# A scan ahead of an out-projection, copies ahead of casts, scans ahead of taps: three reorderings in a two-layer sequence kernel

## The chip, the cores and the metric

The kernel runs on one core of one Trainium2 chip. The metric is the device time of one execution in microseconds (us); of several executions the median is given. Five engines work side by side, each on a queue of its own in strict order: TensorE (PE, matrix products and transposes, with its weight loads shown as PEld), VectorE (DVE), ScalarE (ACT), GpSimd (POOL) and SyncE (SP, which issues the transfers). They wait for each other through semaphores. Operands lie in SBUF; products land in PSUM, which has eight banks here.

## The reference, cut to what matters

Two layers over 2 × 1024 tokens of width 512. Each layer is an attention-like block and a feed-forward block, each with a residual addition and a layernorm behind it:

```python
x = layernorm(x + mamba(x))        # in-projection, 4-tap causal convolution, decayed scan, gate, out-projection
x = layernorm(x + ternary(x))      # out = (x @ W) * scale; out *= tanh(|out|)/|out|, norm held under 0.99
x = layernorm(x + recurrence(x))   # below
x = layernorm(x + swiglu(x))       # (silu(x @ Wg.T) * (x @ Wu.T)) @ Wd.T, integer weights, 512 -> 2048 -> 512
```

The recurrence, in which most of the change lies:

```python
y    = gelu(x @ w_y + b_y)
xb   = x @ w_x + b_x;  conv = conv_b + sum_k conv_w[k] * shift(xb, k)
gx   = sigmoid(conv @ w_ig + b_ig);  ga = sigmoid(conv @ w_ag + b_ag)
a    = exp(-8 * ga * softplus(a_param));  mult = sqrt(1 - a*a)
h[t] = a[t] * h[t-1] + gx[t] * conv[t] * mult[t]
out  = (h * y) @ w_out + b_out
```

## The kernel before, in words

The 2048 tokens are four blocks of 512 (NBLK = 4; two blocks make one sequence, BPS = 2). The width 512 is four pieces of 128 partitions (NK = NJ = 4). A full product for one piece and one block is four instruction pairs of 128×128 by 128×512 that add up in one PSUM bank. The residual stream lies in X[b], 512 tokens × 512 in float32; between layers it also goes out to memory (x_mid, x_lin, x_rec) and comes back by block. Matrix products of the recurrence and of mamba are float32; those of the two feed-forward blocks split each float32 operand in a rounded part and a remainder and multiply both (names wF and lo, wu and wd as the buffers of the ternary block's pieces, hh and hl for the hidden pieces).

The stages come one after the other on TensorE: mamba for blocks 0 to 3 (its in-projection for a block is woven with its out-projection for the one before), the ternary block (`linear`), the recurrence for blocks 0 to 3, then swiglu. A tile scheduler orders the instructions of each engine by their data, by estimated costs and by program order; a few instructions are held in the program's order by hand with `keep_in_program_order`. So a move in the Python text moves instructions only as far as the scheduler follows it.

What the change touches:

- `transposed` (L226): TensorE turns a block of X in four pieces (L237). With `split`, ScalarE writes the rounded piece (L241, the cast to wu) and VectorE the remainder (L242, wd). Without it, and with `by_act`, ScalarE copies the piece (L246, xT).
- `linear` (L946): the ternary block for one token block. It calls `transposed` with `split`, then does the products po (L956), the scale (L960), the norm and its tanh (L962 to L978), the residual addition (L980) and the layernorm (statistics L277 and L278).
- `branches` (L1041): for one block of the recurrence, the products of `product` (L1035) into xpad (L1060), the convolution (L1063, L290) and the gelu branch y. For block 0 it calls `transposed` on X[0], and its steps are woven with those of `linear(2)` and `linear(3)`.
- `gates`: products for both gates, then per piece exp (al, L1090), tanh (ga, L1091), a product on GpSimd (a, L1095; and gx, L1083) and ga on VectorE (L1096).
- `scans`: per piece the root (L1105), gx·ga (L1109), the scan hs (L1111) and y·hs (L1117), all but the root on VectorE. Each piece's y is one of the four operands of every out-projection product.
- `project_back`: per row group j four products po over the four pieces of y (L1123), the sum with the bias on VectorE (r, L1128), the residual addition on GpSimd (x, L1129); for blocks 0 to 2 a layernorm (L277 to L283) and a store of x_rec behind it.
- the last lines of the recurrence: in each round b the gates of block b, then `project_back(b-1)`, then the scans of block b. Behind the last round `gate_up(0)` of swiglu's first group runs on TensorE (L1009), then the first hidden piece (L1019, L1020, L1023, L1024), then `project_back(3)`, then `gate_up(1)` and so on.
- `project` (mamba, L589): steps m = 0 to 8 of the in-projection of a block. `inner(m)` computes a piece and returns a function that runs the four taps of its convolution on VectorE (L290, acc); `scans(4*m - 12)` runs four scans of the decays on VectorE (L570, L), `weigh` one product on VectorE (L580, bdec) and four on GpSimd (L585). The out-projection of the block before (L762) is woven with it.

## Time and profile before

| | |
|---|---|
| median of 3 runs | 1130.05 us (1129.76 to 1130.65) |
| the profiled execution's own time | 1130.25 us |
| its span, first to last instruction | 1128.5 us |
| mean granted TensorE clock | 0.995 |
| busy: TensorE, VectorE, ScalarE, GpSimd | 1104.2, 698.6, 455.6, 362.6 us |
| chain of work that ended last | TensorE 83%, VectorE 11%, ScalarE 3% |

The page of the profile gives busy time by engine, the span in 40 slices, the queues, the chain of work that ended last and the costliest groups of instructions. Other views are cut from the same trace: a timeline lists the instructions of one engine with start, duration, line and the idle time ahead of them with what ended it; the list of waits adds up for one engine what it waited for; windows give busy time of each engine in a stretch with the granted clock. A buffer's name stands in place of its number. "po <- y" reads: the instruction that writes po waited for the one that wrote y.

### The profile page before, as it was taken

Reading aid. Unit: us, or ns where it says so; the run is one execution under the profiler, and the core shown is the slowest. Engines: PE = TensorE matmul, PEld = TensorE weight load, DVE = VectorE, ACT = ScalarE, POOL = GpSimd, SP = SyncE. Lnnn points to the kernel's source line nnn. Section 1 sums busy time; section 2 is a strip of 40 time slices with the busy share of each in tenths; the row PEclk is TensorE's granted clock in tenths of the full one; section 3 lists DMA queues with packets and bytes.
Section 4 is the critical chain, followed back from the end, with each engine's and each line's share of the span. In section 5 each row is a group of like instructions: output and inputs, shape, how many; then the busy total and the mean of one; then the engine's idle time right before and its main releaser. Section 6 shows DMA issues by size and latency. Waiting matters only on the chain.

```text
span 1128.5 us, 12100 instructions
## 1 busy us (share of the span) xinstructions
PE 1104.2 (98%) x4466; PEld 666.0 (59%) x4466; DVE 698.6 (62%) x1262; ACT 455.6 (40%) x694; POOL 362.6 (32%) x347
## 2 busy tenths in 40 slices
PE   8999999999999999999999999989999999999996
PEld 5455445545544655654444444447888887888885
DVE  5979896697779676863717437273238765325224
ACT  3334634452453233566653373642224223224223
POOL 1547471474348240556123231237401001001000
PEclk9999999999999999999999999989999999999999
DMA  8005202701310047158031002203644002100001
GB/s 325 16 14 120 89 1 91 205 0 40 130 53 0 39 172 212 75 112 179 18 37 38 0 1 55 20 37 103 190 91 75 1 1 59 16 1 21 18 1 40
DMA packets 110732, 75.99 MB, mean 67 GB/s; under 512 B 86257, under 2 KB 87057, under 8 KB 108105
## 3 DMA queue, kind: packets, MB, share of 16 engines
q1 hardware_dynamic: 109464, 74.72, 24.9%
q8 instruction: 37, 0.61, 0.2%
q10 hardware_dynamic: 976, 0.39, 0.1%
q14 instruction: 31, 0.25, 0.1%
q0 software_dynamic: 224, 0.02, 0.0%
HBM read 58.91 MB, written 16.02 MB: 66 GB/s over the span
## 4 chain that ended last, share of the span: by engine, by line
PE 83%; DVE 11%; ACT 3%; issue 1%; DMA 1%; POOL 1%; SPq 0%; DVEq 0%; POOLq 0%; ACTq 0%
PE pgu L1009 21%; PE p L1035 18%; PE po L1230 10%; PE pg L364 9%; PE px L364 7%; PE po L1123 5%; PE po L762 4%; PE py L697 2%; DVE L L570 2%; DVE acc L290 2%; PE po L956 2%; PE pxt L666 1%; DVE st L277 1%; DMA cdec<-since 1%; PE py L689 1%
## 5 line engine op out<-in xcount | busy, mean ns | idle before, releaser
L1020 DVE SCALAR_TENSOR_TENSOR h<-pgu,L_ffn_up_scale,sg 128x512 f32<-128x512 f32 x63 | 47.2, 749 | 131.7 <-PE pgu L1009 129.2
L762 PE MATMUL po<-w_out,xc 128*128 128x512 f32 x256 | 112.5, 593 | 2.8 <-DVE L L570 2.8
L364 PE MATMUL px<-xT,w_in 128*128 128x512 f32 x256 | 114.6, 597 | 0.0
L585 POOL TENSOR_TENSOR L<-L,gm 128x512 f32<-128x512 f32 x64 | 93.4, 1488 | 64.8 <-DVE bdec L580 38.3
L364 PE MATMUL pg<-xT,w_in 128*128 128x512 f32 x256 | 113.5, 594 | 0.0
L1035 PE MATMUL p<-xT,w 128*128 128x512 f32 x256 | 112.1, 592 | 1.4 <-ACT xT L246 1.4
L1035 PE MATMUL p<-cv,w 128*128 128x512 f32 x256 | 110.5, 592 | 0.0
L1009 PE MATMUL pgu<-wF__4250,wg 128*128 128x512 f32 x256 | 101.7, 397 | 0.0
L1009 PE MATMUL pgu<-lo__4251,wg 128*128 128x512 f32 x256 | 100.8, 394 | 0.0
L1009 PE MATMUL pgu<-lo__4251,wu 128*128 128x512 f32 x256 | 100.7, 393 | 0.0
L1009 PE MATMUL pgu<-wF__4250,wu 128*128 128x512 f32 x256 | 100.7, 393 | 0.0
L1230 PE MATMUL po<-wd,hl 128*128 128x512 f32 x252 | 98.2, 396 | 0.0
L1230 PE MATMUL po<-wd,hh 128*128 128x512 f32 x252 | 98.2, 395 | 0.0
L1019 ACT ACTIVATE sg<-pgu,L_ffn_gate_scale 128x512 f32<-128x512 f32 x63 | 43.4, 689 | 134.0 <-PE pgu L1009 134.0
L762 PEld LDWEIGHTS po<-w_out,xc 128*128 128x128 f32 x256 | 48.4, 190 | 63.8 <-issue 56.0
L1023 ACT CAST hh<-h 128x512 fp32r<-128x512 f32 x63 | 39.1, 621 | 113.4 <-DVE h L1020 113.2
L1035 PEld LDWEIGHTS p<-cv,w 128*128 128x128 f32 x256 | 48.6, 190 | 61.2 <-issue 59.6
L1035 PEld LDWEIGHTS p<-xT,w 128*128 128x128 f32 x256 | 48.4, 190 | 58.8 <-issue 54.8
L364 PEld LDWEIGHTS px<-xT,w_in 128*128 128x128 f32 x256 | 47.5, 190 | 57.5 <-issue 56.0
L364 PEld LDWEIGHTS pg<-xT,w_in 128*128 128x128 f32 x256 | 47.3, 190 | 54.2 <-issue 53.3
L1348 POOL TENSOR_TENSOR x<-x,r 128x512 f32<-128x512 f32 x12 | 15.1, 1296 | 198.1 <-DVE r L1347 198.1
L290 DVE SCALAR_TENSOR_TENSOR acc<-xpad,cols,acc 128x512 f32<-128x512 f32 x72 | 67.1, 933 | 18.6 <-ACT acc L334 13.8
(288 smaller groups left out, 1928.2 us busy)
## 6 DMA issues: line engine op xcount, KB each, us to landing
L<-decays SPq DMA_DIRECT2D x12, 1024.0 KB, 7.2
x_mid<-x SPq DMA_DIRECT2D x4, 1024.0 KB, 3.8
x<-x_mid SPq DMA_DIRECT2D x4, 1024.0 KB, 6.8
st<-in_L_ffn_gate_w_dram SPq DMA_DIRECT2D x8, 512.0 KB, 4.0
st<-in_L_ffn_up_w_dram SPq DMA_DIRECT2D x8, 512.0 KB, 4.7
st<-in_L_ffn_down_w_dram SPq DMA_DIRECT2D x8, 512.0 KB, 4.2
x_rec<-x SPq DMA_DIRECT2D x4, 1024.0 KB
x<-_attn_hidden_states_dram SPq DMA_DIRECT2D x3, 1024.0 KB
```

The source lines that it names most:

```text
L290: tap = nc.vector.scalar_tensor_tensor(acc, xpad[:, k : k + TB], w[:, k : k + 1], acc, ALU.mult, ALU.add)
L364: nc.tensor.matmul(pm[:n, :], w_in[:, k, lo : lo + n], xT[:, k, :], start=(k == 0), stop=(k == NK - 1),)
L570: nc.vector.tensor_tensor_scan(L[:, h, :], pl, id4.rearrange("p j t -> p (j t)"), 0.0, ALU.mult, ALU.add)
L585: nc.gpsimd.tensor_tensor(L[:, h, :], L[:, h, :], st["gm"], ALU.mult)
L762: nc.tensor.matmul(po, xc[:, m, j * P : (j + 1) * P], w_out[:, m, :], start=(m == 0), stop=(m == NX - 1),)
L1009: nc.tensor.matmul(pm, w[g][:, k, cols], x[:, k, :], start=(k == 0 and x is pieces[0]), stop=(k == NK - 1 and x is pieces[-1]),)
L1019: nc.scalar.activation(sg, pgu[0], AF.Silu, scale=gs[:, m : m + 1])
L1020: nc.vector.scalar_tensor_tensor(h, pgu[1], us[:, m : m + 1], sg, ALU.mult, ALU.mult)
L1023: nc.scalar.copy(halves[0], h)
L1035: nc.tensor.matmul(pm, w1[i][:, k, m * P : (m + 1) * P], rhs[:, k, :], start=(k == 0), stop=(k == NK - 1),)
L1123: nc.tensor.matmul(po, y[:, k, j * P : (j + 1) * P], w1[4][:, k, :], start=(k == 0), stop=(k == NK - 1),)
L1230: nc.tensor.matmul(po[j], x[:, j * P : (j + 1) * P], wd[m // GK][:, m % GK, :], start=(m == 0 and x is h[0]), stop=(m == NF - 1 and x is h ...
```

## The change

Three edits.

1. In the last round of the recurrence (b = 3) the scans of block 3 are called before `project_back(2)` and not behind it. In the other rounds the order stays. (The generator `coming` is in that round `first_pieces`; its steps, which load and split the rows for swiglu's first products, have run inside `gates` by then.)
2. `linear(2)`, the third block of the ternary linear, calls `transposed` with `behind=True`, so that ScalarE's four casts keep their place in program order, behind the copies of X[0]'s pieces for the recurrence's block 0.
3. In mamba's `project` the taps of step m are called behind the four scans and the weighing of this step and not ahead of them.

```diff
-    def transposed(pool, b, X, tags=("xT",), split=False, bufs=1, by_act=False):
+    def transposed(pool, b, X, tags=("xT",), split=False, bufs=1, by_act=False, behind=False):
...
             if split:
-                nc.scalar.copy(xT[:, k, :], pt)
+                copied = nc.scalar.copy(xT[:, k, :], pt)
+                if behind:
+                    tc.keep_in_program_order(copied)
...
         for m in range(3, NX):
-            inner(m)()
+            conv = inner(m)
             if m == 6:
                 spans()
             if m < 7:
                 scans(4 * m - 12)
                 weigh(4 * m - 12)
+            conv()
             yield
...
-            xT = transposed(ep, b, X, tags=("wu0", "wd0") if exact else ("wu0",), split=exact)
+            xT = transposed(
+                ep, b, X, tags=("wu0", "wd0") if exact else ("wu0",), split=exact, behind=b == 2
+            )
...
                 made = gates(b, st["cv"], coming)
+                if b + 1 == NBLK:
+                    scans(b, *made, ys[b])
                 if b:
                     project_back(b - 1, ys[b - 1])
-
-                for _ in range(NK):
-                    next(coming, None)
-                scans(b, *made, ys[b])
+                if b + 1 < NBLK:
+                    for _ in range(NK):
+                        next(coming)
+                    scans(b, *made, ys[b])
                 for _ in coming:
                     pass
```

## The prediction, made before the changed kernel ran

> **What bounds the kernel.** I first read busy time and the slices of the page.

> ```profile
> PE 1104.2 (98%) x4466; PEld 666.0 (59%) x4466; DVE 698.6 (62%) x1262; ACT 455.6 (40%) x694; POOL 362.6 (32%) x347
> PEclk9999999999999999999999999989999999999999
> ```
> ```profile
> PE po L1123 <- DVE y L1117: 3.9, 1, 3.9
> PE po L762 <- DVE L L570: 2.8, 2, 1.9
> PE early L188 <- POOL ident masks.py:199: 1.4, 1, 1.4
> PE p L1035 <- ACT xT L246: 1.4, 1, 1.4
> ...
> PE po L956 <- DVE wd L242: 0.8, 1, 0.8
> ```
> TensorE is busy for 1104.2 of 1128.5 us, so an edit can only give back its idle time or time at a lower clock. The second fence is the list of TensorE's waits (total, times, longest). The whole list holds about 15 us. The largest entry is the last recurrence block's out-projection, which waits for y. The clock row has one dip, in the slice beginning at 26/40 of the span, 734 us. So I read that stretch by windows; the column before the DMA share is the granted clock.

> ```profile
> 741.00:745.00 4.00, 4.00 (x17) 3.00 (x16) 3.32 (x8) 2.70 (x4) 2.54 (x2) 1.00 0.00 0
> 745.00:749.50 4.50, 0.65 (x3) 0.19 (x1) 3.41 (x8) 0.86 (x1) 2.23 (x1) 0.93 0.00 0
> 749.50:757.00 7.50, 7.46 (x11) 3.13 (x12) 7.50 (x13) 0.30 (x1) 0.00 (x0) 0.59 0.00 0
> 757.00:764.00 7.00, 7.00 (x18) 3.17 (x17) 4.47 (x8) 1.90 (x2) 2.50 (x2) 1.00 0.40 150
> ```
> TensorE is idle, and behind the gap it runs at a clock of 0.59 on average; the raw rows have 0.5 from 748.89 to 755.72. The list has no second dip inside the span: waits of 1.9 and 1.4 us left the clock at 1.0, one of 3.9 us halved it.

> VectorE's timeline (start, duration, line, last the idle time before it) tells why y is late:

> ```profile
> 737.56 3.08 DVE L1096 SCALAR_TENSOR_TENSOR ga<-a,ga 128x512 f32<-128x512 f32 x2 [1.96 <-ACT ga L1091]
> 740.57 1.28 DVE L1128 TENSOR_TENSOR r<-po,L_attn_b_out 128x512 f32<-128x512 f32 x2
> ...
> 745.86 1.25 DVE L1111 TENSOR_TENSOR_SCAN hs<-al,last,gx 128x512 f32<-128x512 f32 x1
> 748.20 0.69 DVE L277 BATCH_NORM_STATS2 st<-x 128x6 f32<-128x512 f32 x1 [1.09 <-POOL x L1129]
> 748.81 0.67 DVE L1117 TENSOR_TENSOR y<-y,hs 128x512 f32<-128x512 f32 x1
> ...
> 750.66 0.67 DVE L1109 TENSOR_TENSOR gx<-gx,ga 128x512 f32<-128x512 f32 x1
> 751.24 0.68 DVE L1117 TENSOR_TENSOR y<-y,hs 128x512 f32<-128x512 f32 x1
> 751.84 1.28 DVE L1111 TENSOR_TENSOR_SCAN hs<-al,last,gx 128x512 f32<-128x512 f32 x1
> ```
> ```profile
> 738.37 1.72 POOL L1129 TENSOR_TENSOR x<-x,r 128x512 f32<-128x512 f32 x1
> 741.33 2.54 POOL L1129 TENSOR_TENSOR x<-x,r 128x512 f32<-128x512 f32 x2 [1.23 <-DVE r L1128]
> 745.93 2.23 POOL L1129 TENSOR_TENSOR x<-x,r 128x512 f32<-128x512 f32 x1 [2.07 <-DVE r L1128]
> ```
> Between the gates (ga) and the first y, VectorE does block 2's epilogue: r, statistics, waits for GpSimd's residual adds. Nothing of that is needed by the matmuls that wait.

> **Part 1: scans ahead of block 2's project_back.** The built instruction order shows the move is real. VectorE's new order is ga1, hs0, ga2, ga3, y0, gx1, gx2, hs1, hs2, y1, y2, gx3, hs3, r0, y3, and only then r1 to r3, the statistics and the rest of block 2's epilogue. TensorE keeps its order (gate_up(0), 16 products of block 3's out-projection, gate_up(1)), and ScalarE keeps its own up to the gates and roots, so ga1 to ga3 begin as now: ga3 at 738.89, and it ends near 739.58 (its 1.76 us in the chain of waits were beside GpSimd's add at 738.37, which now comes later; alone it takes 0.69, as ga1 did). From one start to the next a gx, y or r takes 0.59 us and a scan 1.19 (750.66, 751.24, 751.84, 753.04 above). From 739.50: seven of the first kind and three scans, 7 × 0.59 + 3 × 1.19 = 7.7, so y3 starts at 747.2 and ends at 747.9. y0 ends near 740.2, y1 near 744.3, y2 near 744.9.

> TensorE ends gate_up(0) at 745.49. One such product is two instructions of 0.429 us, 0.859 at full clock, so the first chain needs y0 at 745.49, y1 at 746.35, y2 at 747.21, y3 at 748.07: all are there, y3 by 0.2 us. The bound on the bad side: block 2's r0 is out at 747.2, and GpSimd's add begins beside y3. An addition beside such an add took up to 1.76 us instead of 0.68 (rows L747 and L290 go from 0.68 and 0.75 to 1.76). Then y3 ends at 748.95 and TensorE stops for 0.9. But the scan at 745.86 began just ahead of the add at 745.93 and kept its 1.25, while the add stretched to 2.23; y3 too begins just ahead. I take 0.1, nearest to that row.

> So the 16 products take 13.74 us from 745.49 and gate_up(1) starts at 759.23 to 760.1, I take 759.35. Before, they began at 749.53 and gate_up(1) at 766.03: 16.50 us of which 2.76 were the halved clock. Gain: 4.04 of gap + 2.76 of clock − 0.1 = **6.7**.

> [...]

> What is late next: block 2's epilogue (4 r, 4 adds of 1.27, statistics) ends near 753 to 756 instead of 750 to 756, beside some 13 us of out-projection that needs none of it. Its store of x_rec[2] is read by a later group with about 10 us to spare. With TensorE 6.7 earlier, the first hidden pieces (hh, hl) of the next group are ready between 767.7 and 768.5 and due at 768.4 to 768.6; the next weights' conversions are ready at 777.2 and due at 778.1. Cover is thin: below nothing it can't cost, above it is bounded by one more add of GpSimd (1.3). I take 0.2, as the ready times lie at the edge.

> **Part 2: linear(2)'s four casts (L241) behind branches(0)'s xT copies.** ScalarE now casts two (461.70 to 462.65), copies xT four times to 464.71, then casts two. TensorE starts p at 463.30 after 1.41 us of waiting. With the copies first, xT piece 0 ends 0.95 earlier and p starts at 462.3. But the order of po and p on TensorE changes with it: all four subtractions wd (L242, 0.66) fall behind the four x additions (L980, 2.74) and the statistics on VectorE, which end near 468.7; wd of piece 0 ends at 469.3, TensorE is there at 468.8. New wait 0.5 to 0.6, and 0.1 to 0.3 on the pieces behind. Net gain −1.0 + 0.75 = **0.25**; between 1.0 (the wait is covered) and −0.3 (wd pieces each late). The 0.8 wait for wd later in the same loop stays: its chain moves with it. GpSimd's two gx products go behind eight weight conversions; both sets end at 530.4 as before, cover from a continuous queue, so nothing.

> **Part 3: taps behind scans in mamba's project.** Three blocks, no instruction added. TensorE's order and waits are the same. One step's taps (0.73 each) come behind its scans, the group's last scans and its weighing up to 1.3 earlier, the convolved piece up to 1.3 later. The two waits of this stage (0.8 at 127.0 and 1.9 at 143.0) are for scans (L570) which have the same operations ahead of them on VectorE in the new order. Value 0; bounds +2.8 (both waits go) and −1.5 (0.5 per block, if a late convolution holds up TensorE's transposes).

> **Sum.** −6.7 + 0.2 − 0.25 + 0 = −6.75 against the profiled execution's own 1130.25 (span 1128.5 and 1.75 around it). It lies 0.2 over the median 1130.05, inside 1129.76 to 1130.65, so the same difference from the median gives 1123.3. I say **1123.4**.

> **Rivals.**
> - *The stall moves* (0.19): y3 is pushed by the add (0.9) and hh/hl or the converted weights are late once or twice by 1.3, or part 2 costs. Gain 3.3 to 5.5, 1124.5 to 1126.8. For it: the margins of 0.2 and 0.1 us above. Against: GpSimd's adds are late, not long.
> - *Mamba's waits go too* (0.07): gain up to 2.8 more, 1120.5. For it: both waits are for scans, which the change means to advance. Against: the same operations stand ahead of these two.
> - *The clock drops again* (0.08): TensorE stays idle at y3 or at hh for more than the 1.9 us that left the clock alone. An idle time of 2.0 and 2.8 of halved clock come on top of the forecast, 1123.4 + 4.8 = 1128.2, or 1127 with less of it. [...]
> - *The epilogue is starved* (0.06, slower): VectorE runs block 2's statistics, block 3's r and the first hidden piece in one strict row, each waiting for an add of GpSimd. If each of the eight adds took 2.23, as the one beside a scan, and not 1.27, the row would be 7.7 us longer, and hh for gate_up(1)'s followers is late by some 7: all of the gain is given back and the clock drops (2.8), 1133. It decides from 6.7 us of lateness on. Against: only scans stretched an add so, and these come earlier now.
> - That the change does nothing is excluded for part 1 by the order, and it is my forecast for part 3.

> **Chances.** Forecast 0.60 (1121.8 to 1124.5). The range 1120.0 to 1127.0 takes in the first two rivals and leaves about 0.14 outside, nearly all above. A measurement of this kernel can tell about 0.2%, 2.3 us, from no change; faster by more than that 0.90, same 0.04, slower 0.06.

> **What would show it.** Right: no wait po <- y over 0.5 us, clock 1.0 from 741 to 764, the out-projection in 13.7 us, gate_up(1) near 759. Part 2: p's wait near 0.4 and a new po <- wd wait of 0.5. Part 3: the two L570 waits unchanged. Wrong: any wait of TensorE over 2 us between 745 and 785, or a second dip of the clock.

## The result

The changed kernel takes 1125.54 us (median of 6 runs, 1124.79 to 1126.07) against 1129.90 before (6 runs, 1129.01 to 1130.65): ratio 0.996, 95% interval 0.9948 to 0.9973. A second set of five runs (full_again, at the end of the experiments) gave 1125.15, ratio 0.9957 (0.9943 to 0.997). So it is 4.4 and 5.2 us faster, where 6.75 was forecast; the time lies inside the range, 2.1 over the value. One execution of the kernel called stats_last below took 1149.0 us at a mean granted clock of 0.947, where its five others had 0.997 or 0.998; it is left out of the median given there.

### The profile page after: what moved, and what is told of

Same layout as the page of the kernel before. It is cut to its first block, busy times and chain, and to the rows that moved or that the text cites. A ratio compares the mean times of both kernels' runs of the same rounds, so it can differ in the third digit from the quotient of the medians.

```text
span 1123.6 us, 12100 instructions
## 1 busy us (share of the span) xinstructions
PE 1104.9 (98%) x4466; PEld 666.1 (59%) x4466; DVE 698.2 (62%) x1262; ACT 455.5 (41%) x694; POOL 361.2 (32%) x347
## 4 chain that ended last, share of the span: by engine, by line
PE 83%; DVE 10%; ACT 4%; POOL 1%; issue 1%; DMA 1%; SPq 0%; DVEq 0%; ACTq 0%; POOLq 0%
PE pgu L1015 20%; PE p L1041 17%; PE po L1239 10%; PE pg L366 9%; PE px L366 8%; PE po L765 8%; PE po L1129 2%; PE py L700 2%; PE po L962 2%; PE pxt L669 1%; DVE st L279 1%; DVE L L572 1%; POOL x L1135 1%; DVE acc L292 1%; DVE x L986 1%
## 5 line engine op out<-in xcount | busy, mean ns | idle before, releaser
L765 PE MATMUL po<-w_out,xc 128*128 128x512 f32 x256 | 114.2, 600 | 2.6 <-DVE L L572 2.6
L1239 PE MATMUL po<-wd,hh 128*128 128x512 f32 x252 | 98.3, 396 | 0.4 <-POOL wg L911 0.4
L1239 PE MATMUL po<-wd,hl 128*128 128x512 f32 x252 | 98.3, 396 | 0.2 <-DVE hl L1030 0.2
L765 PEld LDWEIGHTS po<-w_out,xc 128*128 128x128 f32 x256 | 49.0, 192 | 64.8 <-issue 56.8
```

What stands on the lines that cost most here:

```text
L765: nc.tensor.matmul(po, xc[:, m, j * P : (j + 1) * P], w_out[:, m, :], start=(m == 0), stop=(m == NX - 1),)
L1239: nc.tensor.matmul(po[j], x[:, j * P : (j + 1) * P], wd[m // GK][:, m % GK, :], start=(m == 0 and x is h[0]), stop=(m == NF - 1 and x is h ...
```

## The profile after

The profiled execution took 1125.38, its span is 1123.6. First the clock row of the page, then TensorE's waits. The changed kernel's line numbers are up to nine higher: L765 is L762 of before, L962 is L956, L1129 is L1123, L1239 is L1230.

```profile
PEclk9999999999999999999999999999999999999999
```
```profile
PE po L765 <- DVE L L572: 2.6, 2, 2.4
...
PE po L962 <- DVE wd L244: 0.8, 2, 0.6
PE p L1041 <- ACT xT L248: 0.6, 1, 0.6
...
PE po L1239 <- POOL wg L911: 0.4, 1, 0.4
...
PE po L1239 <- DVE hl L1030: 0.2, 1, 0.2
```

The wait po <- y is gone from the list and the dip at slice 26 from the clock. What is new: the longer of the two waits for scans grew from 1.9 to 2.4, and two waits appear at the first down-projections (L1239). The last recurrence block by windows (granted clock ahead of the DMA share) and TensorE's timeline:

```profile
741.00:745.00 4.00, 4.00 (x14) 2.46 (x13) 4.00 (x6) 2.67 (x4) 0.00 (x0) 1.00 0.00 0
745.00:749.50 4.50, 4.50 (x16) 2.54 (x14) 4.46 (x8) 0.69 (x1) 0.66 (x1) 1.00 0.00 0
749.50:757.00 7.50, 7.50 (x19) 3.43 (x19) 6.57 (x14) 1.33 (x2) 5.31 (x5) 1.00 0.00 0
```
```profile
746.82 14.02 PE L1129 MATMUL po<-w,y 128*128 128x512 f32 x32
760.27 0.79 PE L1015 MATMUL pgu<-wF__4250,wg 128*128 128x512 f32 x1
```

The windows show no idle time of TensorE there. The 16 products begin the moment gate_up(0) ends and take 13.45 us to gate_up(1), instead of 20.54 from 745.49 to 766.03: 7.09 less. VectorE's rows show the order that was read from the built program, y0 at once behind the gates:

```profile
738.89 2.00 DVE L1102 SCALAR_TENSOR_TENSOR ga<-a,ga 128x512 f32<-128x512 f32 x2 [1.36 <-ACT ga L1097]
740.82 0.68 DVE L1123 TENSOR_TENSOR y<-y,hs 128x512 f32<-128x512 f32 x1
...
748.10 0.67 DVE L1134 TENSOR_TENSOR r<-po,L_attn_b_out 128x512 f32<-128x512 f32 x1
748.68 0.68 DVE L1123 TENSOR_TENSOR y<-y,hs 128x512 f32<-128x512 f32 x1
```

But gate_up(0) itself ends 1.33 later than before. To see where each part acts I compared the start of the matmul with the same number in both traces, counted from the first instruction on. A minus is earlier than before; "second profile" is that of full_again:

| stage (time before, us) | full change | second profile of it | part 1 alone | part 2 alone | part 3 alone | parts 1 and 2 |
|---|---|---|---|---|---|---|
| opening (60) | +0.12 | +0.05 | +0.05 | +0.21 | +0.07 | +0.04 |
| at mamba's 1st wait (128) | -0.48 | +0.05 | -0.55 | -0.38 | +0.07 | +0.05 |
| at its 2nd wait (142) | -0.06 | +0.45 | -0.54 | -0.39 | +0.48 | +0.05 |
| right behind it (150) | +1.64 | +0.45 | +1.15 | +1.31 | +0.48 | +0.05 |
| in the ternary block (455) | +1.66 | +0.73 | +1.06 | +1.21 | +0.74 | +0.07 |
| behind linear(2) (515) | +1.33 | +0.97 | +1.07 | +1.52 | +0.71 | -0.19 |
| gate_up(1) (766) | -5.76 | -6.12 | -6.01 | +0.75 | -0.07 | -7.28 |
| 785 | -4.75 | -5.12 | -4.98 | +0.72 | -0.10 | -6.23 |
| last matmul | -4.84 | -5.22 | -5.02 | +0.65 | -0.06 | -6.17 |

Read down a column; the steps are what counts. Part 1 is a step of -7.1 in every kernel that has it, and behind it a step back of +1.0. Part 3 is +0.4 at the second wait and, in the second profile and alone, +0.3 more up to 455. And there is a step of +1.7 at 143 us in three kernels, two of which don't contain part 3. A step of -0.6 at 128 us stands in three columns too, with and without part 3, so it is not the edits'; its cause stays open. (The 0.8 that parts 2 and 3 alone gain between 515 and 766 are the gap of before with the clock halved for 3.4 us instead of 6.8, 1.4 by the clock records, less a wait of 0.6 for y3 that the faster products run into.)

## The experiments

My theory after this profile: part 1 does what was forecast, 1.0 comes back at the first down-projections, and part 3 lengthens the wait at 143 us past what the clock bears. The rival: the halved clock at 143 us is not part 3's, it comes with some executions of every kernel.

**Each part alone.**

```diff
 # p1_alone: before, with only
+                if b + 1 == NBLK:
+                    scans(b, *made, ys[b])
                 if b:
                     project_back(b - 1, ys[b - 1])
 # p2_alone: before, with only
+                xT = transposed(..., split=exact, behind=b == 2)
 # p3_alone: before, with only
-            inner(m)()
+            conv = inner(m)
...
+            conv()
 # p12: the first two
```

> Part 1 alone: block 3's scans ahead of block 2's project_back, the rest as before. Theory: the gap and the halved clock at 745 us go (7.1 us by the two traces), and 1.0 comes back where the next group's products wait for the hidden piece hh near 770 us; mamba keeps its waits of 0.8 and 1.9 at full clock. 1129.9 - 7.1 + 1.0 = 1123.8, faster than the full change by 1.7. Rival: the longer wait and the halved clock at 143 us in the changed kernel are not part 3's but come with some executions of any of these kernels; then some of these runs show a mean clock of 0.995 to 0.997 and 1125.0 to 1126, others 0.998 and 1124.

Measured: 1124.22, ratio 0.9948 (0.9935 to 0.9962). Its profiled execution, 1125.21, has the halved clock at 143 us without part 3, as the rival says.

> Part 2 alone: linear(2)'s casts behind the xT copies. Both theories: TensorE's wait for xT falls from 1.4 to 0.5 or 0.6, a wait for wd of 0.4 in all comes in its place, 0.26 gained by the traces: 1129.6, not to be told from before.

Measured: 1129.58, ratio 0.9998 (0.9989 to 1.0007). No difference that can be measured.

> Part 3 alone: mamba's taps behind the scans. Theory: VectorE's taps fall beside GpSimd's products, TensorE waits about 0.4 longer at 143 us, the wait passes what the clock bears, and one stretch of 3.4 us at 0.5 costs 1.7: 1131.5, slower than before by 1.6. Rival: part 3 costs nothing by itself, the drop of the clock at 143 us depends on where the execution happens to stand: 1129.9 in the runs without it, 1131.5 in those with it, and before has such runs too.

Measured: 1131.08 against 1130.33, ratio 1.0007 (0.9998 to 1.0016). Its profiled execution has no halved clock, in spite of the longer wait.

> Parts 1 and 2 without part 3. Theory: 1129.9 - 7.1 + 1.0 - 0.3 = 1123.5, 2.0 faster than the full change. Rival: no faster than the full change in runs of the same mean clock: 1124.8 at 0.998, 1125.4 to 1126 below.

Measured: 1124.07, ratio 0.9951 (0.9938 to 0.9965). Its three runs at a mean clock of 0.998 took 1123.94 to 1124.07, those of the full change at that clock 1124.79 to 1125.30 in two other sets. So the rival of this run fails: without a halved clock too the full change is 0.7 to 1.4 slower, though not by the 2.0 of the theory.

Where the clock was halved and where it was not shows in p2_alone, whose mamba is that of before, and p3_alone. TensorE's timeline and the windows around the second wait, first p2_alone, then p3_alone:

```profile
142.58 3.80 PE L764 MATMUL po<-w_out,xc 128*128 128x512 f32 x5 [1.95 <-DVE L L572]
```
```profile
143.40:146.80 3.40, 3.40 (x5) 1.35 (x4) 3.37 (x5) 0.17 (x1) 2.62 (x2) 0.51 0.00 0
```
```profile
143.45 2.84 PE L763 MATMUL po<-w_out,xc 128*128 128x512 f32 x6 [2.36 <-DVE L L570]
```
```profile
143.50:147.00 3.50, 3.50 (x9) 1.59 (x10) 3.46 (x5) 2.00 (x4) 1.95 (x2) 1.00 0.00 0
```

Behind an idle time of 1.95 the clock was 0.51 for 3.4 us in p2_alone; behind one of 2.36 in p3_alone, and behind 1.95 in before, it was 1.0. So my threshold theory falls. The clock records show where to look: within an execution their changes lie whole multiples of 3.413 us apart (in before 6.83 = 2 × 3.413 and then 368.64 = 108 × 3.413; in the full change 136.53 = 40 × 3.413 after the first full clock; in p2_alone 604.16 = 177 × 3.413 between two drops). I cut the idle time by stretches of 3.413 us laid from these changes, called windows here. The table has the idle time in a window and the clock in the next:

| kernel, window | TensorE idle in it | clock in the next |
|---|---|---|
| before, 745.5 to 748.9 | 3.24 | 0.5 |
| full change, 140.3 to 143.7 | 2.37 | 0.5 |
| p1_alone, 139.6 to 143.0 | 1.95 | 0.5 |
| p2_alone, 140.1 to 143.5 | 1.95 | 0.5 |
| before, 141.3 to 144.7 | 1.65 | 1.0 |
| p3_alone, 139.2 to 142.6 | 1.53 (the rest of the 2.36 falls in the next) | 1.0 |
| second profile of the full change, 138.9 to 142.3 and the next | 1.28 and 1.08 | 1.0 |
| taps_later_gate (below), 433.7 to 437.1 | 1.89 | 1.0 |

Idle time is counted here with the ends of matmuls as the profile models them. The place of the windows differs from execution to execution (141.3 to 144.7 in before, 140.3 to 143.7 in the full change). The two waits of 2.36 that lay in two windows each, with at most 1.53 in one (p3_alone and the second profile of the full change), left the clock at 1.0. My estimate from these rows is that a wait of 1.95 to some 3.8 us (twice 1.89) halves the clock only in some executions of one and the same kernel. The rival holds, with one addition that is an estimate from the same rows: part 3 makes the wait 0.4 longer (2.36 for 1.95), and 1.95 of a longer wait fall in one window more often.

Where part 3's own 0.4 us come from shows in VectorE's rows of p3_alone ahead of the third group's scans:

```profile
134.84 0.86 DVE L290 SCALAR_TENSOR_TENSOR acc<-xpad,cols,acc 128x512 f32<-128x512 f32 x1
135.62 0.41 DVE L580 TENSOR_TENSOR bdec<-L,tk 128x256 f32<-128x256 f32 x1
135.96 0.74 DVE L290 SCALAR_TENSOR_TENSOR acc<-xpad,cols,acc 128x512 f32<-128x512 f32 x1
136.62 0.68 DVE L277 BATCH_NORM_STATS2 st<-x 128x6 f32<-128x512 f32 x1
137.23 1.15 DVE L290 SCALAR_TENSOR_TENSOR acc<-xpad,cols,acc 128x512 f32<-128x512 f32 x1
```

The number of operations ahead of these scans is as before, as the prediction had it, but two of the taps take 0.86 and 1.15 instead of 0.73. Each begins while one of GpSimd's four products of the group (L585) runs (133.89 to 135.15, 136.17 to 137.83). In before the taps stood singly between scans, and each began 0.04 ahead of such a product:

```profile
130.76 0.73 DVE L290 SCALAR_TENSOR_TENSOR acc<-xpad,cols,acc 128x512 f32<-128x512 f32 x1
```
```profile
129.19 6.99 POOL L585 TENSOR_TENSOR L<-L,gm 128x512 f32<-128x512 f32 x4 [12.15 <-DVE bdec L580]
137.30 4.95 POOL L585 TENSOR_TENSOR L<-L,gm 128x512 f32<-128x512 f32 x4
```

There the tap kept its 0.73 and the products paid: four of them took 6.99, where the next four, with no tap beside them, took 4.95. In these rows the one of the two that began second took longer.

**The time that comes back at 770 us.** The list names GpSimd's conversion of wg. VectorE's timeline of the changed kernel says something else:

```profile
758.15 0.69 DVE L279 BATCH_NORM_STATS2 st<-x 128x6 f32<-128x512 f32 x1 [1.16 <-POOL x L1135]
...
759.55 2.88 DVE L285 TENSOR_SCALAR x<-x,mv,rs 128x512 f32<-128x512 f32 x4
...
765.03 0.69 DVE L279 BATCH_NORM_STATS2 st<-x 128x6 f32<-128x512 f32 x1 [1.32 <-POOL x L1135]
...
767.93 0.69 DVE L279 BATCH_NORM_STATS2 st<-x 128x6 f32<-128x512 f32 x1 [1.41 <-POOL x L1135]
768.66 0.18 DVE L280 BATCH_NORM_AGGREGATE mv<-st 128x2 f32<-128x6 f32 x1
768.75 0.74 DVE L1026 SCALAR_TENSOR_TENSOR h<-pgu,L_ffn_up_scale,sg 128x512 f32<-128x512 f32 x1
```

The hidden piece h, whose product ended at 764.35, stands behind block 3's statistics, and these wait for GpSimd's additions. Block 2's normalisation (759.55) is in the same row, behind block 3's first statistics. ScalarE's cast hh follows at 769.53 and ends at 770.15, TensorE's po starts at 770.30, where the product before it would have let it start at 769.79. The wait for hl behind it makes up most of the rest of the 1.0. The test holds these statistics in program order, which is behind the first five h:

```diff
-            nc.vector.bn_stats(st, x[:, j, :])
+            taken = nc.vector.bn_stats(st, x[:, j, :])
+            if pinned:
+                tc.keep_in_program_order(taken)
...
-                        layernorm(X[NBLK - 1], engine=nc.gpsimd)
+                        layernorm(X[NBLK - 1], engine=nc.gpsimd, pinned=True)
```

> Parts 1 and 2, and block 3's four statistics (bn_stats of X[3]) held behind the first hidden pieces h in VectorE's order. Theory: the 1.0 us lost near 770 us is h standing behind these statistics, each of which waits for an addition of GpSimd; with them out of the way h is ready as soon as its product, both waits of the products with wd near 770 go, 1124.0 - 1.0 = 1123.0. Rival: the wait is for GpSimd's conversion of wg, as the list of waits names it; then nothing changes, 1124.0.

Measured: 1123.22, ratio 0.9946 (0.9932 to 0.9959).

> The kernel of hh_first once more beside it: 1123.2 within 0.5 by the theory, 2.0 below the full change; by the rival (the gain was the chip's or the execution's) 1124 to 1125.

Measured: 1122.83, ratio 0.9939 (0.9926 to 0.9952). The timed intervals overlap that of parts 1 and 2 without this edit (0.9938 to 0.9965), so the gain is read from the trace: hh_first stands 7.11 ahead of before at 766 us and 7.11 at 785, nothing comes back. Both waits at L1239 are gone, the one put down to wg too.

That alone does not clear wg, as GpSimd's conversions of it end 5 us earlier in hh_first (765.20 for 770.23). But po reads wd and hh, not wg, and in the six traces that have this wait its weight load starts 0.104 to 0.106 behind the signal of the cast hh, and 0.011 to 0.031 behind that of wg. The fixed distance is the one to hh, so the name in the list was wrong. h now follows its product:

```profile
759.57 1.27 DVE L1135 TENSOR_TENSOR r<-po,L_attn_b_out 128x512 f32<-128x512 f32 x2
763.27 0.75 DVE L1027 SCALAR_TENSOR_TENSOR h<-pgu,L_ffn_up_scale,sg 128x512 f32<-128x512 f32 x1 [2.43 <-PE pgu L1016]
```

**Can mamba's waits be ordered away?** First by taps still later, which was meant to leave three fewer ahead of each group's scans, on top of parts 1 and 2. (VectorE runs three of the four taps of a step; the first is ScalarE's, L334.)

```diff
-        inner(2)()
+        held = inner(2)
         yield
         for m in range(3, NX):
-            inner(m)()
+            conv = inner(m)
...
+            held()
+            held = conv
             yield
+        next(g, None)          # in taps_later_gate only
+        held()
```

> Parts 1 and 2, and in mamba's project each step's taps one step later still (behind the next step's scans), so that three taps fewer stand ahead of each group's scans. Theory: VectorE is the bound between 124 and 160 us; both waits of TensorE for scans in block 1 go (2.8 us), and about as much comes back where TensorE next needs VectorE's taps, the transposes pxt and the products py near 160: 1124.0 within 0.5, with the halved clock at 160 if that wait is over 1.9. Rival: only the order holds TensorE up; the waits go for good, 1124.0 - 2.8 = 1121.2.

Measured: 1137.2, ratio 1.0071 (1.0057 to 1.0085).

> As the one before, and one of the gate's products (3.44 us of TensorE that need nothing of VectorE) moved from behind these transposes to ahead of them. Theory: it fills the wait that came back at 160, 1124.0 - 2 to 2.8 = 1121.2 to 1122, less what its absence costs further back in the stage. Rival: the stage is bound by VectorE to its end and the wait comes back once more, 1124.0.

Measured: 1144.68, ratio 1.0129 (1.0113 to 1.0144).

Both theories missed by 13 us and more. The wait at 143 us didn't go, it grew to 4.8 and halved the clock for two windows. VectorE, ScalarE and GpSimd of taps_later:

```profile
139.12 1.64 DVE L292 SCALAR_TENSOR_TENSOR acc<-xpad,cols,acc 128x512 f32<-128x512 f32 x1
140.68 0.74 DVE L782 SCALAR_TENSOR_TENSOR x<-po,rms,x 128x512 f32<-128x512 f32 x1
...
142.28 4.54 DVE L572 TENSOR_TENSOR_SCAN L<-pl,id 128x512 f32<-128x512 f32 x4
```
```profile
140.79 0.63 ACT L342 ACTIVATE xc<-acc 128x512 f32<-128x512 f32 x1 [4.39 <-DVE acc L292]
141.33 2.13 ACT L566 COPY pl<-L 128x512 f32<-128x512 f32 x4
```
```profile
129.25 4.94 POOL L587 TENSOR_TENSOR L<-L,gm 128x512 f32<-128x512 f32 x4 [12.16 <-DVE bdec L582]
135.21 6.68 POOL L587 TENSOR_TENSOR L<-L,gm 128x512 f32<-128x512 f32 x4 [0.42 <-issue]
```

The edit did not do what it was made for: in the order that VectorE ran, the scheduler left 15 taps of block 1 ahead of the third group's scans, as many as in before. Only their places changed: the last five come in a row behind the second group's scans and not among them, four of them beside GpSimd's products. There they take up to 1.75 us each, while a scan L takes 1.18 to 1.22 at any place. Six taps take 7.2 us instead of 4.4, and the third group's scans start at 142.28 instead of 139.48. So these two runs say nothing on what fewer taps would give. In blocks 2 and 3 another 4.3 and 4.1 are lost, in part at the same scans. There ScalarE has a share too: its copies pl, which the scans read, stand in its queue behind the silu xc, which waits for the last of these taps, and VectorE waits 0.52 for them; in block 1 the first copy ended at 141.91, before VectorE was free for it.

Then by the other work ahead of these scans: two statistics of block 0's first layernorm (0.69 + 0.18 each) stand right before them. On top of hh_first:

```diff
 # stats_later
-        layernorm(X[b])
+        layernorm(X[b], pinned=b == 0)
 # stats_last
-        layernorm(X[b])
-        nc.sync.dma_start(x_mid[b], X[b])
+        if b:
+            finish(b)
+
+    def finish(b, pinned=False):
+        layernorm(X[b], pinned=pinned)
+        nc.sync.dma_start(x_mid[b], X[b])
...
         gate(b, st)
+        if b == 1:
+            finish(0, pinned=True)
```

> Parts 1 and 2, X[3]'s statistics behind the first hidden pieces, and besides it the four statistics of block 0's first layernorm (two of them stood ahead of mamba's third group of scans in block 1) held in program order, so that 1.7 us of VectorE leave the way of these scans. Theory: TensorE's wait at 143 us falls from 1.95 to about 0.3; being under 1.9 of any 3.41 us it can halve the clock in no execution, so all runs show 0.997 or 0.998 and a narrow spread; 1123.2 - 1.6 = 1121.6, less up to 1 us if the statistics hold up dtx further back. Rival: VectorE is the bound of the stage and the 1.6 come back at the transposes near 160, 1123.2.

Measured: 1125.53, ratio 0.9965 (0.9952 to 0.9979). The wait at 143 went as forecast (1.4 earlier behind it), and 3.2 were lost at 173:

```profile
173.42 0.64 PE L389 MATMUL pbc<-xT,w_bc 128*48 128x256 f32 x4 [2.03 <-issue]
```
```profile
170.78 1.92 DVE L287 TENSOR_SCALAR x<-x,mv,rs 128x512 f32<-128x512 f32 x4
172.61 2.48 DVE L270 STREAM_TRANSPOSE xT<-xT 128x512 f32<-128x512 f32 x4
```

The list calls that wait "issue"; it is the transposes of block 2's input, which now stand behind the layernorm. That the runs would be narrow was wrong: they reached from 1125.23 to 1128.31. The new wait of 2.03 is itself over 1.95, so by the estimate above it can halve the clock where it falls in one window; in the profiled execution it lies in two (1.11 and 0.92), and whether it did so in the slower runs is not shown.

> As stats_later, but block 0's first layernorm (statistics, root, normalisation and store) as a whole behind block 1's gate, ahead of block 2's taps, where VectorE's timeline has some 4 us of idle time for TensorE's products. Theory: the wait at 143 us stays at about 0.3 to 0.5, and what stats_later lost at 165 to 180 us (3.2 us, the transposes of block 2's input behind the statistics) does not come: 1123.2 - 1.5 = 1121.7. Rival: its 4.9 us of VectorE push block 2's first scans, and TensorE waits there: 1123 to 1125.

Measured: 1121.61 (five runs), ratio 0.9922 (0.9909 to 0.9935): 1.43 gained against before at 142 us and still there at 485, and no halved clock between the ends of the profiled execution. TensorE's list has for the scans

```profile
PE po L766 <- DVE L L574: 1.3, 2, 0.8
```

This is the fastest kernel of the study, 8.8 us under before. At last the full change again, beside stats_later:

> The full change once more, on the chip of the kernel beside it: 1125.4 within 0.5. By the clock's windows its wait of 2.4 us at 143 us halves the clock in somewhat over half of the executions (a window of 3.41 us must hold 1.95 of it), so the runs fall into two groups about 1.7 apart, near 1124.6 with a clock of 0.998 and near 1126 below it. Rival: the spread is noise without groups.

Measured: 1125.15, ratio 0.9957 (0.9943 to 0.997); four runs at 1125.03 to 1125.30 with a mean clock of 0.998 and one at 1126.09 with 0.997. That fits two groups, but 1.0 apart and not 1.7, and with one run of five in the upper: five runs don't settle the share.

## Why the prediction was right, and where it was off

- **What bounds.** Right: TensorE's idle time and its clock were all that could be won, and the last recurrence block's po <- y was the largest piece.
- **Part 1, the gap and the clock: 6.7 forecast, 7.09 measured.** The order of VectorE read from the built program is what ran. y3 began 0.16 ahead of GpSimd's add and kept its 0.68, as chosen from the row of the scan. The 0.1 set aside for it was right: y3 ended at 749.36, and the fourth product's two instructions start 0.45 and 0.53 behind the ones before them and not 0.429, a delay of 0.13. The rest is a slip in the clock's term. The 16.50 of before end at gate_up(1)'s first record, which starts 0.03 behind the last product's second instruction, while 13.74 counts that instruction in full. Read in the same way the products take 13.33 at full clock, so the halved clock had cost 3.16 and not 2.76: 4.04 + 3.16 - 0.13 = 7.07, the 7.09 but for rounding.
- **What is late next: 0.2 forecast, 1.0 measured.** This is the largest mis-sized term. The place was right and so was the bound of 1.3, but the ready time was not: hh was due at 769.79 and ready at 770.15, hl at 770.88, where the forecast, moved by the 1.33 that gate_up(0) ended later, has both by 769.8. VectorE's row behind the scans was taken for shorter than it is. Block 2's epilogue ended at 762.4, where the forecast moved likewise has 754 to 757, as block 3's first r and statistics stand between its own operations; and three of block 3's four statistics wait for an addition of GpSimd. hh_first holds the statistics back and the 1.0 is gone.
- **Part 2: 0.25 forecast.** The xT wait fell from 1.4 to 0.6, where 0.4 was worked out, and a new wait for wd of 0.2 and short stalls between products took all of that again: from 455 to 485 us no kernel with this part gains or loses 0.1. The later wait for wd, which I held for unchanged at 0.8, was 0.55 in the first profile of the full change and 1.05 in the second, so the part comes out between 0.3 gained and 0.3 lost in any one profile, and p2_alone can't be told from before. Without this part the profiles show no such difference; why executions with it differ stays open.
- **Part 3: 0 forecast, 0.6 to 0.7 lost by the profiles** (+0.68 from 128 to 455 us in the second profile of the full change, +0.67 in p3_alone); the timed ratio of p3_alone, 1.0007, reaches to no loss. By the runs at one clock parts 1 and 2 without it are 0.7 to 1.4 faster. The step that failed is "the same operations ahead": the same in number, not in time, because the two taps that began beside a running product of GpSimd took 0.86 and 1.15 in p3_alone and not 0.73.
- **The rival "the clock drops again"** got 0.08 for the wrong place. In the first profile it cost 1.7 at 143 us; the prediction held that 1.9 us leave the clock alone, from a single execution. A wait of 1.95 left it at 1.0 in before, and 0.5 followed one of 1.95 in p1_alone and in p2_alone.
- **Sum.** Without the halved clock: +0.05 + 0.68 + 0.24 - 7.09 + 1.00 - 0.10 = -5.22, the second profile's end. With the halved clock in part of the executions the medians are 4.4 and 5.2 lower. The 1.5 that this falls short of 6.75 are 0.8 for h at 770 us, 0.7 for part 3 and 0.5 for part 2, less 0.4 that part 1 gave beyond its forecast and 0.1 at both ends; so one slip hid part of the others. The time of 1125.5 lies above the band of the forecast itself (1121.8 to 1124.5), in that of the rival "the stall moves" (1124.5 to 1126.8, at 0.19). That rival has the lateness of hh and hl, but neither part 3's loss nor the clock at 143 us, so that the total fell in its band is partly luck.

## What to carry to other kernels

When a stall on the critical engine is removed, walk the next strict queue to its end: here the epilogue that was pushed behind the scans met the next stage's first operation, and pinning four statistics gave 1.0 us back. Count operations ahead of a wait in time and not in number (in p3_alone a tap took 1.15 beside a product of GpSimd and not 0.73), and look at what GpSimd runs beside them and which of the two begins first. Where an order is changed by hand, read the built order to see that the scheduler followed (taps_later left as many taps ahead as before), and ask which other queue copies data for the operation that is moved ahead (ScalarE's pl behind its silu).
